# Pairwise outer products with batch norm: the order of the rows, the cut of their stores, and the store of the last sample

## The chip, the cores and the metric

The kernel runs on one core of a Trainium2 chip. The metric is the device time of one launch in microseconds (us); six runs of the kernel before lie between 1881.48 and 1882.54 us, with a median of 1881.66 us. A core has five instruction streams that matter here: TensorE (PE), VectorE (DVE), ScalarE (ACT), GpSimd (POOL) and SyncE (SP). SP computes nothing; it waits for semaphores and issues the stores. The data are moved by 16 DMA engines.

## What is computed

Two inputs of 1024 samples, 39 fields and 16 numbers each, are combined for all 741 pairs (row, column) with column < row. Cut to what matters:

```python
rows, cols = np.tril_indices(39, k=-1)                      # 741 pairs
cross = xj[:, rows, :, None] * xi[:, cols, None, :]         # 1024 x 741 x 16 x 16
mean = jnp.mean(cross, axis=(0, 2, 3)); var = ...           # one per pair
out = ((cross - mean) * rsqrt(var + 1e-5) * gamma + beta) * W   # W is 16 x 16
```

The output has 1024 x 741 x 256 f32 numbers, 777 MB; the inputs have 6 MB. Row r has r pairs, which lie side by side in the output of a sample: a run of r times 1024 bytes.

## The kernel before, in words

Sample number is partition times 8 plus t, with 128 partitions and t from 0 to 7. A **tile** is one row r for two samples per partition (t0 and t0 + 1): 2 x r x 256 numbers in each partition. The list `tiles` (L67 to L74) fixes the order by hand: row 19 four times (t0 = 0, 2, 4, 6), and then for r = 20, 21, ... 38 and each t0 the tile of row r followed by the tile of row 38 - r. The two together always have 38 rows' worth of pairs, so the output buffer `y_sb` is cut into two halves (slots) that are used in turn: a slot holds one such **round** of 9.96 MB while the other is being filled. A stage of four rounds is spent on each r (for r = 38 there is no partner, and a round is one tile).

Everything is recorded in a fixed order (`manual_schedule`). For each tile number n (L516 to L526): POOL scales xi for tile n + 2 (`scale_xi`, L167); `finish(n)` applies the shift and the weights and issues the stores; then `products(n + 1)` makes the outer products of the next tile, 16 per sample, 11 to 12 of them on ACT and 4 to 5 on POOL (L145, L147), first for the first sample, then for the second. A product overwrites the slot, so it waits for the store that read this place two rounds ago. In `finish` DVE does one instruction for each pair and both samples (L284) over nearly all pairs; POOL takes a share of 13%, or 8 pairs when r is over LONG = 33, where ACT adds their shift (L268) and POOL multiplies in two groups of four (L273).

The first tile is normalized in another way (`weigh`), the first eight are stored in pieces of their own (FIRST_PIECES). `bounds` cuts a later tile's columns into two pieces when r is over ONE = 24, and leaves it whole otherwise. `store` issues what is ready on SP's queue: for a whole tile one transfer with both samples; for a row over 24 one transfer with both samples of the first half of the columns, and then one transfer for each sample of the second half. A transfer is a set of runs, one for each partition and sample, each contiguous in memory; the trace shows one DMA packet for each run. The kernel ends when all stores have landed (SP's wait, L550).

Scale and shift of the pairs are computed on 39 partitions and spread to 128 by matmuls into PSUM; `apply` brings a group of rows into `st_sb` on DVE when the loop reaches the tile number given in ROW_GROUPS. Rows of up to SHORT = 4 pairs have their products on DVE, from a copy of xj in PSUM (L526).

SP's stores carry eight semaphores in rotation: in the built program each transfer on SP's queue waits, before it is issued, for the semaphore that the transfer eight places earlier counts up when it has landed, as well as for the engines that made its data.

Of the kernel before, what the change touches and what calls it, by code (L numbers as in the profile page):

```python
# [14 lines left out]
T = 2  # L15


ONE, LONG = 24, 33
FIRST_PIECES = (
    (0, 1, 3, 6, 10, 14, 19), (0, 4, 9, 14, 19), (0, 4, 11, 19), (0, 9, 19), (0, 10, 20), (0, 9, 18), (0, 10, 20), (0, 9, 18)  # L20
)
# [6 lines left out]

SHORT, OWN = 4, 2


ROW_GROUPS = (
    (19, 20, 0, None), (20, 21, 1, None), (15, 19, 1, 2), (21, 25, 2, 4), (1, 15, 2, 8), (25, 32, 3, 16), (32, 39, 4, 24)
)
SHORT_GROUP = 4


@with_exitstack
def tile_pair_outer_batchnorm(
# [15 lines left out]
    nc = tc.nc  # L55
    P = nc.NUM_PARTITIONS
    NB, F, E = xi.shape
    NT = NB // P
    EE = E * E
# [6 lines left out]
    mid = (F - 1) // 2  # L66
    tiles = [(mid, t0, t0 // T * half // 2) for t0 in range(0, NT, T)]  # L67
    slot = 0
    for r in range(mid + 1, F):
        for t0 in range(0, NT, T):  # L70
            tiles.append((r, t0, slot * half))
            if r < F - 1:
                tiles.append((F - 1 - r, t0, slot * half + T * r))
            slot ^= 1  # L74
# [18 lines left out]
    out_v = out.rearrange("(p t) o n i j -> p t (o n i j)", t=NT)  # L93
# [7 lines left out]
    def scratch(part, parts, *shape):  # L101
        size = 1
        for n in shape:
            size *= n
        at = place[part]
        place[part] = at + size
        assert place[part] <= stop[part]
        ap = flat[0:parts, at : at + size]
        if len(shape) == 2:
            ap = ap.rearrange("p (a b) -> p a b", b=shape[1])  # L110
        elif len(shape) == 3:
            ap = ap.rearrange("p (a b c) -> p a b c", b=shape[1], c=shape[2])
        return ap
# [11 lines left out]
    k, q1, q2, q3, uv, uv_2, v_half, mixed, low, mean, rstd, inv = (scratch("rest", F, F) for _ in range(12))  # L125
# [9 lines left out]
    def view(n):  # L135
        r, _, u = tiles[n]
        return y_sb[:, u : u + T * r, :].rearrange("p (t n) e -> p t n e", t=T)
# [23 lines left out]
    def scale_xi(n):  # L161
        r, t0, _ = tiles[n]
        if r <= SHORT:
            return
        n0 = first[r]
        xs = scaled.tile([P, T, r, E], F32, tag="xs", name=f"xs_{r}_{t0}")
        nc.gpsimd.tensor_tensor(  # L167
            xs,
            xi_sb[:, t0 : t0 + T, 0:r, :],
            s_sb[:, :, n0 : n0 + r, :].to_broadcast([P, T, r, E]),  # L170
            ALU.mult,
        )
        xs_of[n] = xs

    def products(n):

        r, t0, _ = tiles[n]
        if r <= SHORT:
            xs = scaled_short.tile([P, T, r, E], F32, tag="xs_short", name=f"xs_{r}_{t0}")
            nc.vector.tensor_tensor(  # L180
                xs,
                xi_sb[:, t0 : t0 + T, 0:r, :],
                s_short[:, first[r] : first[r] + r]
                .unsqueeze(1)
                .unsqueeze(3)
                .to_broadcast([P, T, r, E]),
                ALU.mult,
            )
            for t in range(T):
                nc.vector.tensor_tensor(  # L190
                    view(n)[:, t].rearrange("p n (i j) -> p n i j", j=E),
                    xs[:, t].unsqueeze(2).to_broadcast([P, r, E, E]),
                    xj_short[:, t0 + t, r - 1 : r, :].unsqueeze(3).to_broadcast([P, r, E, E]),
                    ALU.mult,
                )
            return
        xs = xs_of.pop(n)
        split = E - (POOL_I_FIRST[n] if n < 3 else POOL_I_LONG if tiles[n][0] > LONG else POOL_I)
        for t in range(T):
            for i in range(E):  # L200
                product(n, nc.scalar if i < split else nc.gpsimd, t, i, xs[:, t])

    def store(n, c0, c1, t_from=0, t_to=T):
        r, t0, _ = tiles[n]
        n0 = first[r]

        step = 1 if r > ONE and c1 == r else t_to - t_from
        for t in range(t_from, t_to, step):
            nc.sync.dma_start(  # L209
                out_v[:, t0 + t : t0 + t + step, (n0 + c0) * EE : (n0 + c1) * EE],  # L210
                view(n)[:, t : t + step, c0:c1, :].rearrange("p t n e -> p t (n e)"),
            )
# [34 lines left out]
    def finish(n):  # L247


        r = tiles[n][0]  # L250
        n0 = first[r]
        y = view(n)
        long = r > LONG
        p1 = r // 2 if long else r
        if long:
            share = POOL_PAIRS_LONG
        elif RAW < n < 10:
            share = POOL_PAIRS_FIRST
        else:
            share = int(r * POOL_SHARE + 0.5) if r > SHORT else 0  # L260
        p0 = p1 - share
        step = POOL_PAIRS_LONG // 2 if long else r
        for c0 in range(p0, p1, step):
            c1 = min(c0 + step, p1)
            for c in range(c0, c1):
                t_c = t_sb[:, n0 + c : n0 + c + 1]
                if long:
                    nc.scalar.activation(y[:, :, c, :], y[:, :, c, :], AF.Identity, bias=t_c)  # L268
                else:
                    nc.gpsimd.tensor_scalar(  # L270
                        y[:, :, c, :], y[:, :, c, :], t_c, 1.0, ALU.add, ALU.mult
                    )
            nc.gpsimd.tensor_tensor(  # L273
                y[:, :, c0:c1, :],
                y[:, :, c0:c1, :],
                w_sb.unsqueeze(1).to_broadcast([P, T, c1 - c0, EE]),
                ALU.mult,
            )

        size = 1 if n == RAW else T  # L280
        for t in range(0, T, size):
            for c0, c1 in zip(bounds(n), bounds(n)[1:]):
                for c in [*range(c0, min(c1, p0)), *range(max(c0, p1), c1)]:
                    stt(  # L284
                        y[:, t : t + size, c, :],
                        y[:, t : t + size, c, :],
                        t_sb[:, n0 + c : n0 + c + 1],
                        w_dve.to_broadcast([P, size, EE]),
                        ALU.add,
                        ALU.mult,  # L290
                    )
                store(n, c0, c1, t, t + size)

    with tc.manual_schedule():
# [180 lines left out]
        def spread(group):  # L475
            r0, r1, bank, _ = ROW_GROUPS[group]
            n0, n1 = first[r0], first[r1 - 1] + r1 - 1
            at = used[bank]
            used[bank] = at + 2 * (n1 - n0)
            ps = ps_st[bank][:, at : used[bank]].rearrange("p (x n) -> p x n", x=2)  # L480
            for r in range(r0, r1):
                nc.tensor.matmul(  # L482
                    ps[:, :, first[r] - n0 : first[r] - n0 + r],
                    pick[:, r, :],
                    stq[:, :, 0:r],
                    start=True,
                    stop=True,
                )
            spread_of.append((ps, n0, n1))

        def apply(group):
            ps, n0, n1 = spread_of[group]
            nc.vector.tensor_mul(ps[:, 1], ps[:, 1], st_sb[:, 0, n0:n1])
            if group == SHORT_GROUP:

                nc.vector.tensor_mul(ps[:, 0], ps[:, 0], st_sb[:, 0, n0:n1])
                nc.vector.tensor_copy(st_sb[:, 0, n0:n1], ps[:, 0])
            else:
                nc.vector.tensor_mul(st_sb[:, 0, n0:n1], ps[:, 0], st_sb[:, 0, n0:n1])
            nc.vector.tensor_add(st_sb[:, 1, n0:n1], ps[:, 1], st_sb[:, 1, n0:n1])  # L500
# [8 lines left out]
        for group in range(1, len(ROW_GROUPS)):  # L509
            spread(group)  # L510
        s_short = spread_of[SHORT_GROUP][0][:, 0]
        apply(1)
# [3 lines left out]
        for n in range(1, len(tiles)):  # L516
            if n + 2 < len(tiles):
                scale_xi(n + 2)
            finish(n)
            for group, (_, _, _, tile_of) in enumerate(ROW_GROUPS):  # L520
                if n == tile_of:
                    apply(group)
            if n + 1 < len(tiles):
                products(n + 1)
            if n == 32:
                nc.scalar.copy(xj_short, xj_sb[:, :, 1 : SHORT + 1, :])  # L526


# [26 lines left out]
```

## Time and profile before

| | us |
|---|---|
| median of six runs | 1881.66 |
| the profiled execution | 1881.08 |
| its span, first to last instruction | 1879.4 |
| DVE busy | 1720.4 (92%) |
| ACT busy | 1642.9 (87%) |
| POOL busy | 1531.8 (82%) |
| PE busy | 26.0 (1%) |
| SP's last wait, for the stores in flight | 15.2 |

The page divides the span into 40 slices and gives for each the share of busy time of each engine and of the 16 DMA engines; its third part gives the DMA queues with their packets, bytes and the time that their packets took, as a share of 16 engines over the whole span. The view of waits names, for each line of the kernel, what ended its idle time. The view of stretches gives, for any stretch of time, the busy time of each engine, the share of DMA time and the rate. A landing is the moment when the last of a transfer's 16 parts has counted up its semaphore; the trace has the time of each part, and of each packet its start, length and bytes.

### The profile page before, as it was taken

Reading aid. Unit: us, or ns where it says so; the run is one execution under the profiler, and the core shown is the slowest. Engines: PE = TensorE matmul, PEld = TensorE weight load, DVE = VectorE, ACT = ScalarE, POOL = GpSimd, SP = SyncE. Lnnn points to the kernel's source line nnn. Section 1 sums busy time; section 2 is a strip of 40 time slices with the busy share of each in tenths; the row PEclk is TensorE's granted clock in tenths of the full one; section 3 lists DMA queues with packets and bytes.
Section 4 is the critical chain, followed back from the end, with each engine's and each line's share of the span. In section 5 each row is a group of like instructions: output and inputs, shape, how many; then the busy total and the mean of one; then the engine's idle time right before and its main releaser. Section 6 shows DMA issues by size and latency. Waiting matters only on the chain. (4 is left out here: it accounts for less than half of the span.)

```text
span 1879.4 us, 9660 instructions
## 1 busy us (share of the span) xinstructions
PE 26.0 (1%) x130; PEld 23.3 (1%) x130; DVE 1720.4 (92%) x2625; ACT 1642.9 (87%) x3416; POOL 1531.8 (82%) x1746
## 2 busy tenths in 40 slices
PE   5000000000000000000000000000000000000000
PEld 4000000000000000000000000000000000000000
DVE  8999999998999898989898989898999999888885
ACT  8998989898989798989898989898988888888883
POOL 8999888888888788888888878787888777777873
DMA  5999999999999999999999999999999999999999
GB/s 201 386 419 432 424 431 426 427 431 420 430 423 425 425 425 424 424 424 425 424 425 427 424 425 424 416 426 421 424 419 425 422 424 422 424 419 416 425 415 411
DMA packets 63994, 783.63 MB, mean 417 GB/s; under 512 B 4784, under 2 KB 6448, under 8 KB 17072
## 3 DMA queue, kind: packets, MB, share of 16 engines
q1 hardware_dynamic: 62624, 779.72, 98.3%
q10 hardware_dynamic: 1296, 3.29, 0.5%
q14 instruction: 73, 0.60, 0.1%
q8 instruction: 1, 0.02, 0.0%
HBM read 6.00 MB, written 776.99 MB: 417 GB/s over the span
## 5 line engine op out<-in xcount | busy, mean ns | idle before, releaser
L284 DVE SCALAR_TENSOR_TENSOR y_sb<-y_sb,st_sb,w_dve 128x512 f32<-128x512 f32 (+1 forms) x2511 | 1651.0, 739 | 132.1 <-issue 119.6
L145 ACT ACTIVATE y_sb<-xs,xj_sb 128x288 f32<-128x288 f32 (+20 forms) x3194 | 1510.8, 565 | 192.7 <-DMA out_dram<-y_sb 169.0
L147 POOL TENSOR_SCALAR y_sb<-xs,xj_sb 128x416 f32<-128x416 f32 (+29 forms) x1126 | 604.5, 559 | 40.8 <-DMA out_dram<-y_sb 31.3
L273 POOL TENSOR_TENSOR y_sb<-y_sb,w_sb 128x2048 f32<-128x2048 f32 (+3 forms) x155 | 517.1, 3342 | 104.0 <-ACT y_sb L268 94.4
L167 POOL TENSOR_TENSOR xs<-xi_sb,st_sb 128x640 f32<-128x640 f32 (+33 forms) x135 | 183.9, 1362 | 171.5 <-ACT y_sb L145 165.2
L270 POOL TENSOR_SCALAR y_sb<-y_sb,st_sb 128x512 f32<-128x512 f32 x291 | 196.8, 692 | 0.1
L268 ACT ACTIVATE y_sb<-y_sb,st_sb 128x512 f32<-128x512 f32 x160 | 100.2, 708 | 1.9
L190 DVE TENSOR_TENSOR y_sb<-xs,ps 128x1024 f32<-128x1024 f32 (+3 forms) x32 | 24.8, 817 | 0.6
L482 PE MATMUL ps<-y_sb 39*128 39x38 f32 (+37 forms) x76 | 16.5, 398 | 2.8 <-DVE y_sb L468 2.8
L482 PEld LDWEIGHTS ps<-y_sb 39*128 39x128 f32 x76 | 16.3, 329 | 3.1 <-DVE y_sb L468 3.1
L346 ACT ACTIVATE y_sb<-y_sb 128x1248 f32<-128x1248 f32 x8 | 10.0, 1244 | 2.8 <-POOL y_sb L335 2.7
L351 DVE TENSOR_REDUCE y_sb<-y_sb 128x78 f32<-128x1248 f32 x8 | 11.2, 1446 | 0.4 <-ACT y_sb L346 0.4
L145 ACT ACTIVATE y_sb<-xi_sb,xj_sb 128x304 f32<-128x304 f32 x24 | 11.4, 536 | 0.0
L335 POOL TENSOR_TENSOR y_sb<-xi_sb,y_sb 128x1248 f32<-128x1248 f32 x4 | 9.2, 2320 | 2.0 <-ACT y_sb L384 2.0
L232 DVE TENSOR_TENSOR y_sb<-y_sb,w_dve 128x2048 f32<-128x2048 f32 (+4 forms) x6 | 10.7, 1840 | 0.1
L325 DVE TENSOR_REDUCE y_sb<-xi_sb 128x39 f32<-128x624 f32 (+1 forms) x6 | 6.1, 1012 | 3.8 <-DMA xi_sb<-in_r_xi_dram 3.8
L335 POOL TENSOR_TENSOR y_sb<-xj_sb,y_sb 128x1248 f32<-128x1248 f32 x4 | 9.2, 2320 | 0.0
L371 PE MATMUL ps<-y_sb 128*39 128x79 f32 x48 | 8.1, 340 | 15.1 <-DVE y_sb L351 14.9
L225 POOL TENSOR_SCALAR y_sb<-y_sb,st_sb 128x512 f32<-128x512 f32 x8 | 6.4, 812 | 2.1 <-ACT y_sb L145 2.1
L325 DVE TENSOR_REDUCE y_sb<-xj_sb 128x39 f32<-128x624 f32 (+1 forms) x6 | 6.1, 1014 | 0.6 <-DMA xj_sb<-in_r_xj_dram 0.6
L223 ACT ACTIVATE y_sb<-y_sb,st_sb 128x512 f32<-128x512 f32 x9 | 6.5, 802 | 0.2 <-ACT y_sb L145 0.2
L371 PEld LDWEIGHTS ps<-y_sb 128*39 128x39 f32 x48 | 5.8, 177 | 17.1 <-DVE y_sb L351 10.6
(59 smaller groups left out, 35.2 us busy)
## 6 DMA issues: line engine op xcount, KB each, us to landing
out_dram<-y_sb SPq DMA_DIRECT2D x25, 2304.0 KB, 14.5
out_dram<-y_sb SPq DMA_DIRECT2D x12, 4352.0 KB, 15.4
out_dram<-y_sb SPq DMA_DIRECT2D x12, 4096.0 KB, 16.3
out_dram<-y_sb SPq DMA_DIRECT2D x10, 4608.0 KB, 14.6
out_dram<-y_sb SPq DMA_DIRECT2D x12, 3840.0 KB, 17.4
out_dram<-y_sb SPq DMA_DIRECT2D x21, 2048.0 KB, 17.0
out_dram<-y_sb SPq DMA_DIRECT2D x12, 3584.0 KB, 18.1
out_dram<-y_sb SPq DMA_DIRECT2D x12, 3328.0 KB, 18.1
```

The source lines that it names most:

```text
L145: nc.scalar.activation(y, src, AF.Copy, scale=scale)
L147: engine.tensor_scalar(y, src, scale, 1.0, ALU.mult, ALU.mult)
L167: nc.gpsimd.tensor_tensor(xs, xi_sb[:, t0 : t0 + T, 0:r, :], s_sb[:, :, n0 : n0 + r, :].to_broadcast([P, T, r, E]), ALU.mult,)
L190: nc.vector.tensor_tensor(view(n)[:, t].rearrange("p n (i j) -> p n i j", j=E), xs[:, t].unsqueeze(2).to_broadcast([P, r, E, E]), xj_short ...
L268: nc.scalar.activation(y[:, :, c, :], y[:, :, c, :], AF.Identity, bias=t_c)
L270: nc.gpsimd.tensor_scalar(y[:, :, c, :], y[:, :, c, :], t_c, 1.0, ALU.add, ALU.mult)
L273: nc.gpsimd.tensor_tensor(y[:, :, c0:c1, :], y[:, :, c0:c1, :], w_sb.unsqueeze(1).to_broadcast([P, T, c1 - c0, EE]), ALU.mult,)
L284: stt(y[:, t : t + size, c, :], y[:, t : t + size, c, :], t_sb[:, n0 + c : n0 + c + 1], w_dve.to_broadcast([P, size, EE]), ALU.add, ALU.mult,)
L325: nc.vector.tensor_reduce(total[:, t0:t1, part(x)], sources[x][:, t0:t1], AX.X, ALU.add)
L335: nc.gpsimd.tensor_tensor(devs[n % 7], sources[x][:, t0 : t0 + T], shift[:, x : x + 1, :].unsqueeze(3).to_broadcast([P, T, F, E]), ALU.sub ...
L371: nc.tensor.matmul(ps_g[acc][0:F, 0 : 2 * F + 1], lhs, fb[:, t], start=t == 0, stop=t == NT - 1)
L482: nc.tensor.matmul(ps[:, :, first[r] - n0 : first[r] - n0 + r], pick[:, r, :], stq[:, :, 0:r], start=True, stop=True,)
```

## The change

- The order of the rounds becomes: row 19, then 20 with 18, then 38, 37 with 1, 36 with 2, and so on down to 21 with 17. The last tile is row 17, where it was row 38.
- ONE goes from 24 to 30: only rows over 30 are cut into two pieces.
- Rows over 19 (from the ninth tile on) are stored sample by sample. A row over 30 has three transfers: first half of the columns of the first sample, second half of the first sample, and all columns of the second sample. A row from 20 to 30 has two, one for each sample, each a run of the whole row. Rows below 20 stay as they were.
- The very last tile is stored by 21 transfers: its first sample on 128 partitions as one; of its second sample, partitions 16 to 127 as one, and partitions 0 to 15 in 19 small ones of 2 to 16 partitions and 1 to 5 columns.
- The groups of rows that `apply` brings in are cut and placed for the new order (twelve instead of seven), and xj is copied to PSUM at tile 12 instead of 32.

```diff
-ONE, LONG = 24, 33
+ONE, LONG = 30, 33
+FEWER = (2, 3, 4, 6, 8, 12)
 ROW_GROUPS = (
-    (19, 20, 0, None), (20, 21, 1, None), (15, 19, 1, 2), (21, 25, 2, 4), (1, 15, 2, 8), (25, 32, 3, 16), (32, 39, 4, 24)
+    (19, 20, 0, None), (20, 21, 1, None), (18, 19, 1, 2), (38, 39, 1, 8), (34, 38, 1, 9), (1, 5, 1, 10), (29, 34, 2, 36),
+    (5, 10, 2, 37), (25, 29, 3, 76), (10, 14, 3, 77), (21, 25, 4, 108), (14, 18, 4, 109),
 )
-SHORT_GROUP = 4
+SHORT_GROUP = 5
-    for r in range(mid + 1, F):
+    for r in (mid + 1, *range(F - 1, mid + 1, -1)):
         for t0 in range(0, NT, T):
             tiles.append((r, t0, slot * half))
     def store(n, c0, c1, t_from=0, t_to=T):
         r, t0, _ = tiles[n]
         n0 = first[r]
-        step = 1 if r > ONE and c1 == r else t_to - t_from
+        if n == len(tiles) - 1:
+            parts = [(0, P, T - 2, 0, r), (E, P, T - 1, 0, r)]
+            for q, k in enumerate(FEWER):
+                parts += [(0, k, T - 1, 2 * q, 2 * q + 2), (k, E, T - 1, 2 * q, 2 * q + 1)]
+                parts += [(k, E, T - 1, 2 * q + 1, 2 * q + 2)]
+            parts += [(0, E, T - 1, 2 * len(FEWER), r)]
+            for p0, p1, t, c0, c1 in parts:
+                nc.sync.dma_start(
+                    out_v[p0:p1, t0 + t, (n0 + c0) * EE : (n0 + c1) * EE],
+                    view(n)[p0:p1, t, c0:c1, :].rearrange("p n e -> p (n e)"),
+                )
+            return
+        whole = n >= len(FIRST_PIECES)
+        step = 1 if r > mid and (whole or c1 == r) else t_to - t_from
         for t in range(t_from, t_to, step):
+            if whole and step == 1 and t == t_to - 1:
+                if c1 < r:
+                    continue
+                c0 = 0
             nc.sync.dma_start(
-            if n == 32:
+            if n == 12:
                 nc.scalar.copy(xj_short, xj_sb[:, :, 1 : SHORT + 1, :])
```

## The prediction

> **What bounds the kernel now.** I read the slices first, then the DMA queues, the stretches by stage, and SP's waits.
>
> ```profile
> DMA  5999999999999999999999999999999999999999
> GB/s 201 386 419 432 424 431 426 427 431 420 430 423 425 425 425 424 424 424 425 424 425 427 424 425 424 416 426 421 424 419 425 422 424 422 424 419 416 425 415 411
> ...
> q1 hardware_dynamic: 62624, 779.72, 98.3%
> ...
> q14 instruction: 73, 0.60, 0.1%
> ```
>
> The DMA engines are full from the third slice on, at 411 to 432 GB/s. DVE, ACT and POOL are busy 92, 87 and 82%, so none of them is the bound. What can be saved is time per byte, time per packet, or idle time of the DMA engines. The packet records say more: in the landings of one store 12 of the 16 engines agree within 0.2 us, and up to four lag, the last by 4.9 us around 1130 to 1215. The 8 KB packets of the instruction queue take 0.31 us each, and the lag grows in such steps, so I take the four for the engines that also fetch instructions. I call the last one X. From 68 us to its last packet at 1877.95 X has no gap that matters: at 1831.45, where the other engines had run dry for 1.6 us, its next packet starts in the same hundredth. Each end of a store that anybody waits for is X's. So the time is X's bytes and packets, its fetches, and its idle time, now about none.
>
> The next view is that of stretches, cut where the last store of each row's stage lands: rows 21, 22, 23, 24 (two runs for each partition and row tile), then 25 to 29 (four).
>
> ```profile
> 185.30:278.90 93.60, 0.00 (x0) 0.00 (x0) 88.81 (x137) 84.79 (x192) 77.64 (x100) 1.00 1.01 429
> 278.90:372.40 93.50, 0.00 (x0) 0.00 (x0) 87.96 (x136) 84.89 (x192) 77.87 (x101) 1.00 1.00 426
> 372.40:466.00 93.60, 0.00 (x0) 0.00 (x0) 86.95 (x133) 85.38 (x193) 77.87 (x101) 1.00 1.00 426
> 466.00:559.70 93.70, 0.00 (x0) 0.00 (x0) 87.12 (x133) 84.93 (x192) 78.03 (x101) 1.00 1.00 426
> 559.70:654.20 94.50, 0.00 (x0) 0.00 (x0) 86.92 (x133) 84.78 (x192) 77.89 (x101) 1.00 1.01 425
> 654.20:748.20 94.00, 0.00 (x0) 0.00 (x0) 86.96 (x133) 84.77 (x192) 77.96 (x100) 1.00 1.01 425
> 748.20:842.70 94.50, 0.00 (x0) 0.00 (x0) 87.45 (x134) 84.88 (x192) 78.42 (x102) 1.00 1.01 424
> 842.70:936.50 93.80, 0.00 (x0) 0.00 (x0) 86.29 (x132) 84.90 (x192) 77.25 (x100) 1.00 1.01 424
> 936.50:1031.20 94.70, 0.00 (x0) 0.00 (x0) 87.63 (x134) 84.88 (x192) 78.50 (x102) 1.00 1.01 425
> ```
>
> The first number after the stretch is its length. Every stage moves the same 39.85 MB. With two runs it takes 93.60 us in the mean, with four 94.3; over all of rows 25 to 37 (559.67 to 1784.47 in 13 stages) it is 94.22. The 64 more packets for each engine cost 0.62 us, **9.7 ns a packet**; a fit over all full stretches of 10 us gives 10.25.
>
> **Fewer runs.** Rows 25 to 30 go from four packets for each partition and tile to two, rows 31 to 38 to three. That is (6 x 2 + 8) x 4 tiles x 128 partitions = 10,240 packets, 640 an engine, at 10 ns: **-6.4 us** (-6.2 to -6.6). It is all on X, hence on the path. The largest packet now has 24,576 bytes, the changed ones up to 38,912; the time of a packet is straight in its size up to there (87 ns for 2048 bytes, 920 for 24,576). If runs over 32 KB were cut in two, rows 33 to 38 would lose a third of what one row's stage gains, 192 packets an engine or 1.9 us; I take the straight line. In number of transfers the two kernels are alike apart from the end (283 stores, then 299 of which 19 are the small ones).
>
> **Later first piece, earlier first sample.** For a long row the first transfer holds a quarter of the tile instead of a half; for rows 25 to 30 nothing is issued until DVE has done the row. Against this the first sample's place is free after half of the row has been stored instead of three quarters, and ACT, whose largest wait is 169.0 us in 68 pieces for the landing of stores, starts earlier. With u = 0.306 us, the time of one pair and sample in a stage (93.5 / 4 / 76), and B the moment when the previous round of the same slot begins to be stored, the next round of this slot must be under way by B + 46.6.
>
> - Row 29: the second sample's place lands at B + 58u = 17.8; ACT needs 0.5 to start and 6.8 for 12 products; DVE 25 x 0.66 = 16.5; SP to first packet 0.9. Sum B + 42.5, **4 us to spare**. The same sum for before gives B + 36.7 for the first issue, and the trace has B + 36.95 (960.62 to 997.57), so I trust it. Row 30 has 3 to spare, rows below 29 more.
> - Row 38: second sample lands at B + 23.3; ACT 0.5 + 7.7 (half of the 15.34 below); first piece 11.8 later behind POOL's two groups, second at 19.9 behind DVE; 0.9. The first is ready at B + 44.2, in time; the second at B + 52.3, while the first quarter covers until 46.6 + 5.8 = 52.4. **Just even**. Row 37, by the same sum, has 1 us to spare; 36 to 31 have more.
>
> ```profile
> 1826.18 15.35 ACT L145 ACTIVATE y_sb<-xs,xj_sb 128x608 f32<-128x608 f32 x22 [2.57 <-DMA out_dram<-y_sb]
> 1830.27 7.52 POOL L147 TENSOR_SCALAR y_sb<-xs,xj_sb 128x608 f32<-128x608 f32 x10
> 1830.35 32.74 SPq L209 DMA_DIRECT2D out_dram<-y_sb  x6
> 1841.61 19.84 DVE L284 SCALAR_TENSOR_TENSOR y_sb<-y_sb,st_sb,w_dve 128x512 f32<-128x512 f32 x30 [3.18 <-issue]
> ```
>
> This is row 38 now, the last rounds: ACT starts on a landing, DVE on ACT's end, SP on DVE. Where 20|18 goes over to 38, the same chain from the landings at 161.65 and 185.34 has the second piece ready at 191.7 and the first one stored at 191.1: 0.6 us idle. With 0.05 for each of the four tiles, **+0.8 us** (0 to 3; the bound is 0.6 for each of the 38-tiles). Where the row changes, now a larger row waits for the small tile's store too; going down that wait is gone, but X was never idle there, so it is worth nothing.
>
> The groups of `apply` add 1 to 2 us to DVE, spread over the stages, each with about 6 us of DVE idle (93.6 - 87): nothing. The xj copy is one ACT instruction: nothing.
>
> **The end.** Now the last store is 128 x 19 columns x 2 transfers, issued 16 us before it lands, and X works until 0.15 us of the other engines' end. After the change, the last row is 17, its slot's cover is large (16 us by the sum above), and the first two transfers of the last tile queue up with it. But each transfer waits for the one eight places before it. That such a wait holds SP up can be seen at the start, with the loads:
>
> ```profile
> SPq L550 <- DMA out_dram<-y_sb: 15.2, 1, 15.2
> ...
> SPq L303 <- DMA xi_sb<-in_r_xi_dram: 2.5, 2, 1.5
> ```
>
> Of the 19 small transfers six wait for long-landed stores or row 21's, the seventh for the last tile's first sample; the eighth waits for the big one over partitions 16 to 127, that is until X has stored its share. From then 12 transfers are left, and they need SP's time one after another. Back to back, SP's loads at the start follow each other in 0.37 to 0.48 us; I take 0.43. The last one's first packet comes 0.9 after its issue and takes 0.2 (5,120 bytes). So the end is 0.1 + 11 x 0.43 + 0.9 + 0.2 = 5.9 after X's last large packet, where a plain store would have had one more 17 KB packet, 0.66. **+5.3 us**, in which the DMA engines are nearly idle. The other end of the price: in the long rows the second of two back-to-back stores holds SP for 1.23 us (1861.86 is one), 1.3 apart; 11 x 1.3 would make +14.8. Below: if the small ones were all under way in time, the end would cost nothing. I take the loads' row, since there as here the engines' queues are near empty.
>
> [...]
>
> **Sum.** The profiled execution took 1881.08 (0.6 under the median): 1881.08 - 6.4 + 0.8 + 5.3 = **1880.8 us**. About 0.2%, or 3.8 us, is what a measurement tells from no change.
>
> **Rivals.**
>
> - The end costs nothing (0 instead of +5.3): 1875.5, faster. For it: the engines other than X finish some us earlier, and could take the small ones. Against: SP's order. 0.15.
> - SP's price at the end is that of the back-to-back stores: -6.4 + 0.8 + 14.8 gives 1890.3, slower. It decides from 0.85 us a transfer, where the sum passes +3.8. For it: they are stores, not loads. Against: they have at most 16 rows, not 128. 0.13.
> - The long rows run dry: the quarter piece doesn't cover the second one, 0.3 to 1 us for each of the eight tiles of 38 and 37: 1883 to 1889. For it: row 38's sum is even to 0.1 us. Against: the same sum meets before's row 29 within 0.3. 0.12.
> - The change doesn't do what it says: runs over 32 KB are cut or slower: 1882.7. 0.08.
> - The forecast, 1879 to 1883: 0.52.
>
> Faster holds the first rival and a little of the forecast, 0.16; slower the second and half of the third, 0.20; within 0.2% the rest, 0.64. The range leaves out most of the second rival: **1875 to 1888**.
>
> **What would show it.** Some 10,100 packets fewer; stages of 20 to 30 near 93.6 us, of 31 to 37 near 93.9; no gap in DMA around row 38 over 1 us; and at the end about 5 us in which SP issues small transfers while the DMA rate falls to nearly nothing. The forecast is wrong if that gap is missing or twice as long, or if a stage of the long rows takes over 95 us.

## The result, and the profile after

The changed kernel takes **1886.1 us** (median, 1885.8 to 1887.9) against 1881.5 for the kernel before: ratio 1.0026, 95% interval 1.0019 to 1.0032. It is slower, by 4.6 us; the forecast was 1880.8, no change. The profiled execution took 1885.82 us with a span of 1884.1 (before: 1881.08 and 1879.4), so the two spans differ by 4.7.

First the slices and the store queue of the page after, to be read against the same lines of before:

```profile
DMA  5999999999999999999999999999999999999997
GB/s 203 387 419 423 409 422 424 429 426 425 429 425 427 426 426 425 428 426 424 426 423 424 432 423 430 429 424 428 431 428 425 430 427 425 431 428 427 427 428 289
...
q1 hardware_dynamic: 52666, 779.73, 97.7%
```

There are 9,958 packets fewer: 10,240 saved, and 282 net spent, 157 of them on the small pieces and 125 on the packets of 4 bytes that count up semaphores (16 for a transfer in the kernel before: 4,640 for the 290 on SP's queue). In the middle the rate is a little higher than before. Two slices are lower than their neighbours: the fifth (409) and the last (289, before 411). In both the DMA engines stand still for a while, and there the time is lost; not all of the last slice's loss belongs to the small transfers, for the kernel with a plain end (run 1 below) has 349 in it, because there the engines finish up to 8 us apart.

Next the view by stretches, cut where the last store of each stage lands: rows 38, 37, 29 and 28, then the last microseconds.

```profile
185.20:281.50 96.30, 0.00 (x0) 0.00 (x0) 82.21 (x126) 81.51 (x121) 74.89 (x55) 1.00 0.97 416
281.50:375.30 93.80, 0.00 (x0) 0.00 (x0) 84.20 (x135) 79.91 (x121) 73.93 (x53) 1.00 1.00 425
1031.60:1125.40 93.80, 0.00 (x0) 0.00 (x0) 88.48 (x135) 85.47 (x194) 77.81 (x100) 1.00 1.01 429
1125.40:1219.00 93.60, 0.00 (x0) 0.00 (x0) 87.45 (x133) 85.51 (x195) 77.82 (x100) 1.00 1.00 425
1861.90:1872.20 10.30, 0.00 (x0) 0.00 (x0) 0.00 (x0) 0.00 (x0) 0.00 (x0) 1.00 0.67 235
1876.80:1882.60 5.80, 0.00 (x0) 0.00 (x0) 0.00 (x0) 0.00 (x0) 0.00 (x0) 1.00 0.20 36
```

A four-run stage took 94.22 before; these take 93.6 to 93.8, as the packets promised. Row 38 takes 96.3 (93.48 before, where it came last): the DMA engines lose 2.3 us, in the mean of the sixteen, from 190.59 to 193.08. In the last 5.8 us they move 36 GB/s. In the stretch 1861.9 to 1872.2 the packet records show something that no line of the page tells: 43 packets of 17,408 bytes take 0.75 to 1.67 us; most others of that size take 0.65.

X is the prediction's name for the DMA engine that finishes last. For X's landings the texts here, and the prediction's 161.65 and 185.34, take the end of the last packet of a store; the semaphore, by which landings were defined above, counts up some 0.35 to 0.5 us later. By the ends of X's packets the 4.7 us come together so:

| place | predicted, us | measured, us |
| --- | --- | --- |
| up to the end of 20\|18 | 0 | -0.2 |
| stage of row 38 | +0.8, less its packets | +2.9 |
| rows 37 to 25, fewer runs | -6.1 of the -6.4 | -5.6 |
| rows 24 to 21 | 0 | +0.5 |
| long packets in the last tile | 0 | +1.9 |
| small transfers behind X's last large packet | +5.3 | +5.2 |
| sum | -0.3 in all | +4.7 |

### The profile page after: what moved, and what is told of

It is laid out like the page before. It is cut to its first block, busy times and chain, and to the rows that moved or that the text cites. A ratio compares the mean times of both kernels' runs of the same rounds, so it can differ in the third digit from the quotient of the medians.

```text
span 1884.1 us, 9659 instructions
## 1 busy us (share of the span) xinstructions
PE 26.0 (1%) x130; PEld 23.3 (1%) x130; DVE 1723.9 (91%) x2640; ACT 1645.8 (87%) x3416; POOL 1532.3 (81%) x1746
## 4 chain that ended last, share of the span: by engine, by line
DMA 37%; ACT 13%; DVE 7%; issue 1%; POOL 0%; SPq 0%; ACTq 0%; DVEq 0%; POOLq 0%
DMA out_dram<-y_sb 37%; ACT y_sb L149 13%; DVE y_sb L306 7%; POOL xs L171 0%; SPq L231 0%; ACTq L149 0%; DVEq L572 0%; DVE st_sb L522 0%; DVE ps L515 0%; DVE st_sb L521 0%; DVEq L306 0%; POOLq L171 0%
## 5 line engine op out<-in xcount | busy, mean ns | idle before, releaser
L306 DVE SCALAR_TENSOR_TENSOR y_sb<-y_sb,st_sb,w_dve 128x512 f32<-128x512 f32 (+1 forms) x2511 | 1653.2, 739 | 117.2 <-issue 103.9
L149 ACT ACTIVATE y_sb<-xs,xj_sb 128x288 f32<-128x288 f32 (+20 forms) x3194 | 1514.8, 565 | 181.4 <-DMA out_dram<-y_sb 148.6
L151 POOL TENSOR_SCALAR y_sb<-xs,xj_sb 128x480 f32<-128x480 f32 (+27 forms) x1126 | 604.6, 560 | 14.3 <-DMA out_dram<-y_sb 14.2
L295 POOL TENSOR_TENSOR y_sb<-y_sb,w_sb 128x2048 f32<-128x2048 f32 (+3 forms) x155 | 517.6, 3345 | 87.4 <-ACT y_sb L290 77.8
L194 DVE TENSOR_TENSOR y_sb<-xs,ps 128x256 f32<-128x256 f32 (+3 forms) x32 | 24.8, 817 | 0.5
L149 ACT ACTIVATE y_sb<-xi_sb,xj_sb 128x304 f32<-128x304 f32 x24 | 11.4, 536 | 0.0
```

The costliest lines, as they stand in the source:

```text
L149: nc.scalar.activation(y, src, AF.Copy, scale=scale)
L151: engine.tensor_scalar(y, src, scale, 1.0, ALU.mult, ALU.mult)
L194: nc.vector.tensor_tensor(view(n)[:, t].rearrange("p n (i j) -> p n i j", j=E), xs[:, t].unsqueeze(2).to_broadcast([P, r, E, E]), xj_short ...
L295: nc.gpsimd.tensor_tensor(y[:, :, c0:c1, :], y[:, :, c0:c1, :], w_sb.unsqueeze(1).to_broadcast([P, T, c1 - c0, EE]), ALU.mult,)
L306: stt(y[:, t : t + size, c, :], y[:, t : t + size, c, :], t_sb[:, n0 + c : n0 + c + 1], w_dve.to_broadcast([P, size, EE]), ALU.add, ALU.mult,)
```

## The experiments

A dry spell is a time in which the DMA engines have nothing to store. My theory after the result (T): row 38 is late because POOL is late and the first piece is small; the twelve small transfers cost what was forecast; the 112-partition transfer itself lengthens packets; the saved packets are nearly worth their price. The rivals stand with each run. All medians below are of kernels run beside the kernel before (1881.5 to 1881.6 each time).

| kernel | median, us (range) | ratio to before, 95% |
| --- | --- | --- |
| changed kernel | 1886.1 (1885.8 to 1887.9) | 1.0026 (1.0019 to 1.0032) |
| 1 plain end | 1879.4 (1879.0 to 1880.1) | 0.9989 (0.9980 to 0.9998) |
| 2 end in 112 + 16 partitions | 1881.0 (1880.8 to 1881.7) | 0.9997 (0.9988 to 1.0006) |
| 3 nine small transfers fewer | 1884.4 (1884.0 to 1885.7) | 1.0015 (1.0007 to 1.0024) |
| 4 first tile of row 38 in old pieces | 1878.6 (1878.2 to 1879.4) | 0.9984 (0.9975 to 0.9993) |
| 5 order only | 1882.2 (1881.2 to 1883.0) | 1.0003 (0.9994 to 1.0012) |
| 6 pieces only | 1919.1 (1918.4 to 1919.6) | 1.0201 (1.0187 to 1.0215) |
| 7 all of row 38 in old pieces | 1878.5 (1878.2 to 1879.3) | 0.9985 (0.9976 to 0.9994) |
| 8 no POOL share ahead of row 38 | 1878.2 (1877.8 to 1879.1) | 0.9982 (0.9974 to 0.9991) |
| 9 = 8 + first piece of 24 pairs | 1876.2 (1875.7 to 1877.7) | 0.9971 (0.9961 to 0.9982) |
| 10 the 112 partitions alone | 1880.1 (1879.9 to 1881.1) | 0.9993 (0.9984 to 1.0001) |
| 11 end in two halves of 64 | 1882.3 (1882.1 to 1883.4) | 1.0003 (0.9994 to 1.0011) |
| 12 end in two column blocks | 1879.5 (1879.1 to 1880.5) | 0.9989 (0.9980 to 0.9998) |

### The end

**1, plain end.**

```diff
-        if n == len(tiles) - 1:
-            parts = [(0, P, T - 2, 0, r), (E, P, T - 1, 0, r)]
...
-            return
```

> The changed kernel with its last tile stored like every other short row, both samples by one transfer over 128 partitions, and nothing else altered. Theory T (the end costs twice: 5.2 us for the twelve small transfers that SP issues one after another behind the last large packet, and 1.9 us because the 112-partition transfer makes the packets around it longer): 1886.1 - 5.2 - 1.9 = 1879.0 us, no packets over 0.75 us in the last 20 us, and the end within 3 us of the last large packet. Rival R1 (the long packets near the end come from the order of the rows or from the lagging engines, not from the end's transfers): they stay, 1880.9 us. In both, the dry spell of some 2 us in the first tile of row 38 stays.

1879.4, and each of the 204 packets of 17,408 bytes from 1861 us on takes 0.66 us or less. The end as a whole costs 6.7 us (7.1 expected). The dry spell of row 38 stays: 2.3 us.

**2, two transfers instead of twenty.**

```diff
-            for q, k in enumerate(FEWER):
...
-            parts += [(0, E, T - 1, 2 * len(FEWER), r)]
+            parts += [(0, E, T - 1, 0, r)]
```

> The changed kernel with the last sample in two transfers instead of twenty: partitions 16 to 127 by one, as before, and partitions 0 to 15 whole by a second. Theory T (the 112-partition transfer itself makes neighbouring packets longer): the long packets of 0.8 to 1.7 us stay, the chain of small transfers goes: 1886.1 - 5.2 = 1880.9 us, 1.9 over the kernel with a plain end. Rival R2 (the small transfers collide with the large packets): no long packets, 1879.0 us, the same as a plain end. Rival R3 (the sixteen rows of the second transfer land on engines that already lag): 1 to 2 us more than either without any long packet.

1881.0, as T has it. The tail is gone (the last packet of all is X's), which puts the price of the small transfers at 1886.1 - 1881.0 = 5.1 us. The long packets stay, 53 of them, and 1.6 us over the plain end with them. But the longest now take up to 2.95 us, where the changed kernel has none over 1.67; a transfer of sixteen partitions stands beside the one of 112, and this run doesn't yet say which of the two did it.

**3, nine fewer.**

```diff
-FEWER = (2, 3, 4, 6, 8, 12)
+FEWER = (2, 3, 4)
```

> The changed kernel with three cuts instead of six in the last sample, so nine small transfers fewer. Theory T (each small transfer after the seventh costs one more issue of SP, 0.34 us, behind the last large packet): 1886.1 - 9 x 0.34 = 1883.0 us, and some 2.8 us from the last large packet to the last small one instead of 5.9. Rival R4 (the tail is the latency of a small transfer and the wait for eight landings, hardly their number): 1885.5 to 1886.1 us.

1884.4, between the two. What SP waits for in the changed kernel from 1840 us on (L218 stores the last tile; us in total, times, longest):

```profile
SPq L218 <- DMA out_dram<-y_sb: 19.7, 4, 6.3
```

That is the wait for the transfer eight places before, four times. The last of them ends at 1877.08. Behind it twelve transfers follow each other in 0.34 us, 0.35 in the mean; with nine fewer, three. The number of partitions is not what makes them cheap for SP: in the changed kernel the first four of the small transfers, issued from 1851.90 to 1855.38 right behind the two large ones, held SP for 0.99 to 1.21 us each. What differs at 1877 is that the DMA engines have hardly anything left to do, as the prediction had assumed: at each of the twelve 0 to 24 data packets were issued and not yet stored, at those four 343 to 379. The second of two 128-partition stores, too, held SP for 0.42 us at 192.49, in the dry spell of row 38 (128 packets), and for 1.24 at 213.78 (193). In run 3 itself the last of the three carries 11,264 bytes of each of partitions 0 to 15, and these 16 packets take 1.35 to 1.70 us where the straight line through the packet sizes gives 0.42. From X's last large packet to the end it is 3.8 us instead of the expected 2.8. The number of transfers counts as T has it (9 x 0.34 = 3.1), and sixteen neighbouring partitions take back some 1.2: both are needed.

**10, the 112 partitions alone.**

```diff
             parts = [(0, P, T - 2, 0, r), (E, P, T - 1, 0, r)]
-            for q, k in enumerate(FEWER):
...
```

> The last tile's first sample by one transfer of 128 partitions and its last sample by the 112-partition transfer alone; partitions 0 to 15 of the last sample are left out and stay unwritten. Theory T (the 112-partition transfer makes the packets longer by itself): packets of 17,408 bytes of 0.8 to 1.7 us from about 1862 us on, and against the plain end's 1879.4 us one such packet less on each engine (0.65 us) and 1.5 to 1.9 us more: 1880.3 to 1880.7 us. Rival R2 (the long packets of the run with two transfers come from the sixteen partitions that were sent by the second): none over 0.75 us, 1878.8 us.

Here partitions 0 to 15 of the last sample are left out. 1880.1, with 41 long packets, up to 1.71 us. With 0.65 us less to store than the plain end it takes 0.7 more, so the transfer costs X some 1.3 us by itself. R2 falls.

**11 and 12, other cuts of the same sample.**

```diff
-            parts = [(0, P, T - 2, 0, r), (E, P, T - 1, 0, r)]
-            for q, k in enumerate(FEWER):
...
+            parts = [(0, P, T - 2, 0, r), (0, P // 2, T - 1, 0, r), (P // 2, P, T - 1, 0, r)]   # 11
+            parts = [(0, P, T - 2, 0, r), (0, P, T - 1, 0, 8), (0, P, T - 1, 8, r)]              # 12
```

> The last sample by two transfers over partitions 0 to 63 and 64 to 127, no small ones. The runs so far leave open why the 112-partition transfer makes packets longer. [...] Rival R11 (what hurts is that 112 partitions give seven, an odd number, to each engine, or that some engines then work on another transfer): with four each in both halves there are no packets over 0.75 us, 1879.4 us. [...]

> The last sample by two transfers of all 128 partitions, pairs 0 to 7 and pairs 8 to 16. [...]

Halves: 97 long packets and 2.9 us over the plain end. Their median is 1.36 us; 56 of them take 1.2 to 1.4, about twice 0.65, and 11 take 2.4 to 2.73, about four times. Columns: 8,192 bytes in 0.31 to 0.32 and 9,216 in 0.35 to 0.36, no long one, 1879.5 to the tenth. So neither the odd seven, nor the number of transfers, nor small size lengthens packets: **leaving partitions out of a transfer does**, in each cut by partitions that was run (41 long packets with 112 alone, 53 with 112 and 16, 97 with two times 64). Run 3's last transfer, over 16 partitions, is slow itself: 16 x 11,264 bytes between 1879.82 and 1881.67 are 97 GB/s. Why the packets get longer is not shown: no record says which engine reads which partition.

### Order and pieces apart

**5, order only; 6, pieces only** (both with a plain end).

```diff
-ONE, LONG = 30, 33   # 5
+ONE, LONG = 24, 33
...
-    for r in (mid + 1, *range(F - 1, mid + 1, -1)):   # 6
+    for r in range(mid + 1, F):
```

Run 5 has the whole store() of before, run 6 the row groups and the place of the xj copy of before.

> The new order of the rows alone (20|18, then 38 down to 21, with the groups of statistics that go with it), the stores in pieces as before the change (rows over 24 in four runs per partition and tile, both samples of the first half together) and a plain end. Theory T (the stage of row 38 loses 2.9 us only because its first piece is one sample and POOL's products come late; the order costs nothing else, and no packets are saved): 1881.5 us, within 0.5, the stage of row 38 at 94.0 to 94.5 us. Rival R6 (the place of row 38 right behind 20|18 is what costs, whatever the pieces): that stage stays near 96.4 and the time is 1883.5 to 1884.5 us.

> The order of before (20|18, then 21 up to 38) with the new, fewer and longer runs and the last tile stored as its row is. Theory T (the 10,240 packets are worth 5.6 us on the slowest engine in any order; row 38 in pieces of one sample costs about 2.9 us wherever it stands): 1881.5 - 5.6 + 2.9 = 1878.8 us. Rival R7 (the saving needs the new order, since with the long rows last the dry spells at the end take it back): 1881 us or more, with several dry spells over 1 us in rows 36 to 38.

Order alone (with the row groups that go with it): 1882.2, no measurable change, though a little above the 1881.5 within 0.5 that was expected, and row 38 right behind 20|18 takes 94.1 us at the full rate. The stretch of row 38, then of row 29:

```profile
185.40:279.50 94.10, 0.00 (x0) 0.00 (x0) 80.71 (x123) 79.09 (x118) 73.80 (x54) 1.00 1.00 427
1032.80:1127.40 94.60, 0.00 (x0) 0.00 (x0) 88.58 (x135) 85.37 (x194) 78.93 (x102) 1.00 1.01 424
```

R6 falls; the place of the row costs nothing without the pieces. The new pieces on top of this order (run 1 against run 5) are worth 2.8 us: -5.8 in rows 37 to 25 (9.5 ns for each of 608 packets an engine), +2.4 in row 38, +0.8 in rows 24 to 21.

Pieces alone: 1919.1, **37.6 us slower** than before, where I expected 1878.8. Neither T nor R7 had foreseen the size. The losses stand at the changes of row, from row 23 to 24 on, not in rows 36 to 38 alone. The change from row 29 to 30 in the timeline of the pieces alone (128x464 is row 29, 128x480 row 30; SPq L213 issues stores; in brackets the idle time before and what ended it), then the stretch in which the DMA engines pay for it, at a share of 0.23:

```profile
983.63 14.31 ACT L145 ACTIVATE y_sb<-xs,xj_sb 128x464 f32<-128x464 f32 x36 [1.29 <-DMA out_dram<-y_sb]
985.57 27.47 SPq L213 DMA_DIRECT2D out_dram<-y_sb  x6
...
1007.34 15.91 ACT L145 ACTIVATE y_sb<-xs,xj_sb 128x480 f32<-128x480 f32 x30 [9.40 <-DVE y_sb L288]
...
1012.85 2.58 POOL L147 TENSOR_SCALAR y_sb<-xs,xj_sb 128x480 f32<-128x480 f32 x4 [2.85 <-DMA out_dram<-y_sb]
1021.59 2.06 DVE L288 SCALAR_TENSOR_TENSOR y_sb<-y_sb,st_sb,w_dve 128x512 f32<-128x512 f32 x3 [9.07 <-issue]
```

```profile
1034.60:1039.90 5.30, 0.00 (x0) 0.00 (x0) 5.30 (x9) 5.30 (x10) 5.22 (x8) 1.00 0.23 97
```

ACT stands 9.4 us before the first product of row 30. The view names DVE, but DVE had long been at other work. The landings (ends of the last packet, as above) say what it was: the store of row 29's first sample in that half of the buffer lands at 997.99, the one of its second sample at 1006.76, the short row's behind it at 1012.27. ACT starts 0.58 us after the second, and POOL goes on with the second sample 0.58 us after the third. Samples lie one behind the other, T x r places; a first sample of 30 places reaches one place into where the second sample of 29 lay, and that whole sample is now one run that lands 9 us later; the second reaches into the short row's place. Going down, a first sample ends inside its predecessor. So the order is worth nothing by itself, and 40 us where the pieces are the new ones (1919.1 - 1879.4, row groups included). The prediction said of this wait that it is "worth nothing"; that holds for the old pieces only.

### Row 38

The timeline of the changed kernel at this point (POOL L295 multiplies its share of row 18's last tile, L151 and L149 are row 38's products, L306 DVE's pairs):

```profile
162.29 7.73 ACT L149 ACTIVATE y_sb<-xs,xj_sb 128x608 f32<-128x608 f32 x11 [0.84 <-DMA out_dram<-y_sb]
162.37 2.36 POOL L295 TENSOR_TENSOR y_sb<-y_sb,w_sb 128x1024 f32<-128x1024 f32 x1
164.70 7.50 POOL L151 TENSOR_SCALAR y_sb<-xs,xj_sb 128x608 f32<-128x608 f32 x10
172.23 5.01 ACT L290 ACTIVATE y_sb<-y_sb,st_sb 128x512 f32<-128x512 f32 x8 [2.22 <-POOL y_sb L151]
172.23 19.84 DVE L306 SCALAR_TENSOR_TENSOR y_sb<-y_sb,st_sb,w_dve 128x512 f32<-128x512 f32 x30 [2.24 <-POOL y_sb L151]
```

ACT is done at 170.0 and waits with DVE for POOL until 172.2. Four runs tell apart what to make of it, all with the plain end.

```diff
-        whole = n >= len(FIRST_PIECES)
+        whole = n >= len(FIRST_PIECES) and n != 12          # 4
+        whole = n >= len(FIRST_PIECES) and r < F - 1        # 7
...
+        if n == 11:                                         # 8 and 9, in finish()
+            share = 0
...
+        if r == F - 1:                                      # 9, in bounds()
+            return 0, 24, r
```

**4, the first tile in old pieces.**

> The kernel with the plain end, and in the first tile of row 38 alone the first piece holds half of both samples again, as it did before the change, instead of half of one. Theory T (X runs dry there because POOL's ten products hold up both halves, and a first piece of one sample is too small to cover the time until the second): the dry spell of about 2 us goes, some 128 packets per queue come back (0.1 us): 1879.0 - 2.2 = 1876.8 us. Rival R5 (the 2.9 us of that stage come from the late start of the tile, which a larger first piece doesn't bring forward, so that the wait moves ahead of the piece or behind it): 1878.3 to 1879.0 us.

1878.6: only 0.9 us. The spell of 2.3 us at 191 is gone, and one of 1.7 opens at 237.67, in the third tile. R5 is nearer.

**7, all four tiles.**

> The kernel with the plain end, and all four tiles of row 38 (not only the first, as in the run before) with a first piece of half of both samples. Theory T, mended by that run (the first tile's larger piece moved the dry spell to the third tile, because a first sample's store that ends late also frees the buffer late; with all four tiles in the old pieces nothing is left to wait for): the stage of row 38 at 94.0 to 94.5 us, 0.3 us of packets back: 1879.4 - 2.0 = 1877.4 us. Rival R8 (row 38 has no short row beside it, so DVE can't stay ahead whatever the pieces): 1878.3 us or more, dry spells of over 1 us remain in that stage.

1878.5, hardly better than run 4. The stage of row 38 takes 93.8 us, a little under what T says, but row 37 now takes 95.5, with spells of 1.2 us at 284 and 0.7 at 309. My mended theory falls. R8 has the time but not the place: row 38 itself stays fed. It looks as if, where the new pieces begin, the engines must be further ahead of the stores, and as if a larger piece only moved the place where this lead is paid for; run 9 tests that.

**8, POOL relieved.**

> The kernel with the plain end, and in the tile ahead of row 38 (the last of row 18) POOL gets no share of the additions and multiplications; DVE does all 18 pairs. The computation is the same. Theory T (POOL's ten products for row 38 end 2.2 us after ScalarE's because POOL is still at its share of the tile before): POOL starts them some 4 us earlier, ScalarE's own products are last, and the dry spell in the first tile of row 38 shrinks from 2.3 to under 0.5 us: 1877.2 to 1877.6 us. Rival R9 (the spell comes from the size of the first piece, or moves to the next tile): 1878.5 to 1879.4 us.

1878.2, that is 1.3 us, between T's range and R9's. The spell shrinks to 1.8, not to 0.5. The timeline shows that POOL had held up the start, and who is late next (L283 is here POOL's share, L294 DVE's pairs):

```profile
159.98 31.68 DVE L294 SCALAR_TENSOR_TENSOR y_sb<-y_sb,st_sb,w_dve 128x512 f32<-128x512 f32 x48
161.52 7.49 POOL L151 TENSOR_SCALAR y_sb<-xs,xj_sb 128x608 f32<-128x608 f32 x10
162.90 7.72 ACT L149 ACTIVATE y_sb<-xs,xj_sb 128x608 f32<-128x608 f32 x11 [0.87 <-DMA out_dram<-y_sb]
...
173.35 9.03 POOL L283 TENSOR_TENSOR y_sb<-y_sb,w_sb 128x2048 f32<-128x2048 f32 x2 [0.32 <-ACT y_sb L278]
```

DVE no longer waits for anybody: 18 pairs of row 18 and 30 of row 38 without a break until 191.7, when the second piece goes out. The first goes out at 182.41, when POOL's share is done; it is 5.8 us of storing, and the second comes 9.3 us later. DVE is now the late one. The run is not POOL's lateness alone, for POOL's two pairs of row 18 went to DVE, at 0.66 us each: by its 18 pairs from 159.98 on DVE comes to row 38 at about 171.9, 1.2 us after ACT's last product; in the changed kernel it came 2.2 us after.

**9, a first piece of 24 pairs.**

> The kernel before this one (plain end, POOL without a share in the last tile of row 18) and, in the four tiles of row 38, a first piece of 24 of the 38 pairs instead of 19. The computation is the same. Theory T, mended (with POOL out of the way the first piece goes out when POOL's eight pairs are done, at a time when DVE could have done five more pairs; DVE is then the one that is late with the second piece, so a first piece of 24 pairs costs no time and covers 5 x 128 KB / 0.427 MB per us = 1.5 us more): the dry spell of 1.8 us in the first tile falls to about 0.3 us, the one of 0.7 us in the third tile goes: 1878.2 - 2.0 = 1876.2 us. Rival R10 (the lead that runs of a whole sample need has to be built up once and is paid for somewhere, so a spell that is filled here opens in row 37, as it did with other pieces): 1877.7 to 1878.3 us.

**1876.2, as expected to the tenth**, and the fastest kernel of the study: 0.29% under before (0.18 to 0.39), 9.9 us under the changed kernel. The spell is 0.4 us, and row 38's stage and the next are:

```profile
187.30:280.50 93.20, 0.00 (x0) 0.00 (x0) 80.76 (x124) 81.38 (x121) 72.87 (x52) 1.00 1.00 428
280.50:374.30 93.80, 0.00 (x0) 0.00 (x0) 84.62 (x135) 79.95 (x121) 74.19 (x54) 1.00 1.00 425
```

Nothing opens in row 37, R10 falls: the lead is not owed somewhere in any case. POOL's queue and a first piece that was smaller than it could be account for the loss together. What each is worth alone is not shown: a first piece of 24 pairs with POOL's share left in place was not run. As an estimate from the changed kernel, such a piece, 24/19 of 5.8 us from 184.75 on, would last until 192.1, and the second piece starts at 192.9, so most of the spell would go by the piece alone.

## Why the prediction was wrong, point by point

Two steps failed. The chain at the change from 20|18 to 38 left POOL out and gave +0.8 where the stage of row 38 lost 2.9 us, and the sum of the end put the effect of the 112-partition transfer on other packets at nothing, where it cost 1.3 to 1.9 us. The rest of the miss is a saving that came out 0.5 us smaller and 0.5 us in rows 24 to 21 that stay open. The prediction had named the sign itself: a gap of over 1 us at row 38 (2.3) and a stage of the long rows over 95 us (96.3). That its range, 1875 to 1888, holds the 1886.1 is luck: it was that wide for rivals that did not come about as described.

- **Fewer runs, -6.4**: right, a little large. 9.5 ns a packet on X (against run 5) instead of 10 in rows 37 to 25. The rival of runs over 32 KB falls: the packet count is exactly the planned one, the 512 packets of 38,912 bytes take 1.44 us in the median, where the straight line gives an estimated 1.45, and rows 36 and 37 gain 0.46 and 0.42 us like the others.
- **Later first piece, +0.8**: the step that failed first. "Where 20|18 goes over to 38, the same chain from the landings at 161.65 and 185.34 has the second piece ready at 191.7." The chain followed ACT and DVE; POOL's ten products of 7.5 us were not in it, and they stand behind POOL's share of the tile before. DVE starts at 172.2 instead of 170. The sum has a slip besides: the terms shown for row 38 (0.5 + 7.7 + 19.9 + 0.9) lead from 161.65 to 190.7, not 191.7, and so to no idle time at all. With POOL's 2.2 us they give 192.9, which is when the second piece's first packet starts; the first piece ends at 190.7 to 190.9, close to the predicted 191.1. In the spell X loses 2.0 to 2.3 us, and a second one, of 0.7, stands in the third tile, where 0.05 had been allowed. The stage loses 2.9 us against before, 2.4 against the same order with the old pieces; with the 0.3 us of saved packets added back the term is 3.2 or 2.7, at the edge of its stated 0 to 3. The steady sum for rows 29 to 37 was right: no spell over 0.8 us there.
- **The wait where the row changes**: "worth nothing" was right for the numbers asked and wrong as a statement. With the new pieces it is worth some 40 us (run 6).
- **The end, +5.3**: the mechanism was right, and the size by some luck: 0.34 us a transfer instead of 0.43 makes the chain 0.9 us shorter, and a slower last transfer (its packets of 5,120 bytes take 0.39 to 0.74 us instead of 0.2, and they don't start together) and a later start make up for it. From X's last large packet to the end it is 5.88 us; 5.9 was predicted. One small transfer lands 1.3 to 1.5 us after SP begins to issue it (the last one 2.0), and the next is issued 0.34 us later, so they are in flight together. The rivals of a free end and of 1.3 us a transfer fall, the second because the engines have hardly anything left to do by then (0 to 24 packets), not because the transfers are small (run 3).
- **What the end's sum left out, +1.3 to +1.9**: the second step that failed. I took the packets beside the 112-partition transfer at 0.66 us, as in a plain store. Beside a transfer that leaves partitions out packets take up to 1.7 us with 112 partitions and 2.73 with two halves (runs 10 and 11), beside column pieces none is long (run 12). Why that is so is not shown.
- **Rows 24 to 21, +0.5 to +0.8**: not in the sum, and open. X falls back by some 0.7 us a row against the other engines from row 30 down, and at the end of run 1 twelve engines finish at 1868.8 to 1869.1, the others at 1871.4, 1873.2, 1874.6 and 1877.0. Order alone ends with 5.3 us of such lag. No run shows what makes X slow. The instruction fetches that I took for it are 73 in both kernels, which doesn't rule them out: in run 1, from 1003 to 1846 us, the four late engines fall behind the other twelve by 15 us together, and in that time 35 fetch packets take 10.9 us. They could be most of it, not all; the records don't name the engine of a packet.

The rival "the long rows run dry" covers the measured time, but not with its mechanism: it would have cost each tile of rows 38 and 37, and only the first tile of row 38 (2.3 us) and its third (0.7) were dry.

## What to carry to other kernels

Where a store-bound kernel goes to longer runs, ask for each buffer which run now frees it and how late that run lands: order and pieces gave -2.1 us together, +0.7 (within the noise) and +37.6 apart. In a chain of who is ready when, write down every engine that has a share, with what stands before it in its queue. If a last store has to be cut, cut it along the columns and not along the partitions: two pieces by columns cost nothing here, two halves of the partitions 2.9 us, the 112-partition transfer 1.3 to 1.9. And keep the number of transfers behind the last large one small: the twelve cost 5.1 us.

## What the runs showed of the hardware

- Where a store over a part of the partitions is under way, packets of 17,408 bytes get longer: up to 1.7 us instead of 0.65 with 112 partitions (run 10), up to 2.73 with two times 64 (run 11), up to 2.95 with 112 and 16 (run 2); the same bytes over all 128 partitions not at all, in one piece (0.66 or less, run 1) or cut by columns (8,192 bytes in 0.31 to 0.32, 9,216 in 0.35 to 0.36, run 12).
- What an issue right behind another cost SP went with the data packets issued before it and not yet stored: with 0 to 24 of them, at the end of the changed kernel, transfers of 4 to 16 partitions leave SP every 0.34 us; with 343 to 379, right behind the two large stores, small ones take 0.99 to 1.21. The second of two 128-partition stores, between 100 and 1850 us, takes 1.09 to 1.28 in all 57 cases with 200 packets or more, and with under 165 it takes 0.42 to 0.55 in six of eight, 0.94 and 1.07 in the others. In the kernel before all 53 have 200 or more, and take 1.20 to 1.28.
- The DMA engines of one core fell up to 8.2 us apart by the end of run 1 (1868.8 to 1877.0). In the kernel before, where the long rows came last and the other engines ran dry for 1.6 us, up to 1831.45, while X still worked, the last store's 16 parts landed within 0.2 us.
